# Two graph layers on one core: seven block products for eight in the maps of layer 0, and edges counted by fours

## The chip, the cores and the metric

The kernel runs on one core of a Trainium2 chip. The metric is device time in microseconds, of the whole program. A core has five engines that work beside each other, each through its own queue in order: TensorE (PE; its weight loads are PEld), VectorE (DVE), ScalarE (ACT), GpSimd (POOL) and SyncE (SP, which only issues transfers here). An engine that waits holds up all that stands behind in its queue.

## The reference

`x` is 4096 x 512 in float32, `adj` 4096 x 4096 of 0 and 1 in int32 (about one in 128 set). Layer 0, cut to what matters:

```
keep = (A > 0) & (cumsum(A > 0, axis=1) <= 64)        # the first 64 neighbours of a row
cnt  = keep.sum(axis=1)
xj   = leaky_relu((keep @ X) / max(cnt, 1) @ W_nb.T + b_nb)
xi   = leaky_relu(X @ W_line.T + b_line)
x    = layernorm(X + xi + where(cnt > 0, xj, 0))
```

Layer 1 is attention over the same neighbours: `Wh = h @ W + bW`, scores from two dot products of each row of `Wh`, masked by `adj`, softmax over a row, times `Wh`, then added to its input and normed. Each layer's output has the shape of `x`.

## The kernel before

The rows are cut in 32 blocks of 128 (`NB`), the 512 columns in four chunks of 128 (`NC`). The order of instructions on each engine is the order in which the program writes them (`manual_schedule`); the framework only adds waits. Four stages follow each other on TensorE.

*Maps of layer 0* (the loop over `i` in 32 blocks). As `(keep @ X) @ W_nb.T` is `keep @ (X @ W_nb.T)`, both maps are taken first: `linear(xt, "nb")` gives Y = X W_nb.T, `linear(xt, "line")` the term of the row itself, each with four float32 matmuls of 128x128 by 128x512 into a PSUM bank of `ps_acc` (six banks; `ps_s` has two more). `xt` is the transposed block. Its transpose comes from a load in pieces (`load_turned_x`, four transfers on POOL's queue into one of three `c` tiles) and one VectorE transpose (`turn_x`). Y is kept in SBUF for all 32 blocks as two terms: `y_hi`, cast by ScalarE (L413), and `y_lo`, the rest, by VectorE (L435). The row's own term goes through `line` (bias added on VectorE), `bend` (leaky relu on ScalarE) and `own` (x added on VectorE, then stored to `own_d` on POOL's queue). `load_own_x` loads x for it into one of three `xb` tiles, on POOL's queue too.

*Codes.* Beside the maps, `adj` is turned into one byte per edge, in 64 steps of 128 rows by 2048 columns. `load_adj` (SP) brings 1 MB of int32; `edge` (ScalarE, a steep sigmoid) makes it bf16 0 or 1; `scan` (VectorE) keeps how many neighbours a row has left, at least 2 and counting down from 66, and multiplies it by the edge; `pack` (ScalarE) makes bytes and POOL stores them to `code_d`. So a code is 0 for no edge, over a threshold for one of the first 64, and lower for a later one. `count` takes the number of neighbours from the end of the scans. `codes_until` runs these steps beside the maps until `AHEAD` = 20 are done.

*Neighbour sums* (32 blocks by four groups `s`). `load_kt` brings a block's codes transposed, `make_kt` (ScalarE, L254) turns 128x1024 bytes into 0 or 1 in float32r, and 64 matmuls (L521) add `keep @ y_hi` and `keep @ y_lo` in one bank. `finish` norms a block and stores it. `codes_step` and `codes_late` run the other 45 codes here, at `RATE` = 25/16 a block.

*Layer 1*: maps with W (L825), then attention (L739), where products of pairs of blocks are already taken as seven for eight. The change leaves it as it is.

Before the maps, `turn_w` transposes the weights on TensorE, and `fold_w` (ten VectorE steps of 128x512) folds W with the two score vectors.

Of the kernel before, what the change touches and what calls it, by code (L numbers as in the profile page):

```python
# [9 lines left out]
F32 = mybir.dt.float32  # L10
# [10 lines left out]
P = 128  # L21
# [11 lines left out]
def two_layer_adj_gnn(  # L33
# [43 lines left out]
    two, steep, far, neg_half = few[:, 0:1], few[:, 1:3], few[:, 3:4], few[:, 4:5]  # L77
    for k, value in enumerate((2.0, -0.5 * STEEP, -1.5 * STEEP, FAR, -0.5)):
        nc.vector.memset(few[:, k : k + 1], value)
# [57 lines left out]
    with ExitStack() as l0:  # L137
        adj_p = l0.enter_context(tc.tile_pool(name="l0_adj", bufs=2))
        big = l0.enter_context(tc.tile_pool(name="l0_big", bufs=1))
        y_hi = big.tile([P, NB, C], F32R, name="y_hi")  # L140
        y_lo = big.tile([P, NB, C], F32R, name="y_lo")
# [20 lines left out]

        def edge(s):
            if s < NB * NCH:
                b, h = divmod(s, NCH)
                edge_of[s] = adj_p.tile([P, CH], BF16, name="edge")
                nc.scalar.activation(  # L167
                    edge_of[s], loaded.pop(s), AF.Sigmoid, bias=steep[:, 0:1], scale=STEEP,
# [3 lines left out]
        def scan(s):  # L172
            if s < NB * NCH:
                b, h = divmod(s, NCH)

                left = adj_p.tile([P, CH], BF16, name="left")
                e = edge_of.pop(s)
                end = ends[:, b : b + 1]
                nc.vector.tensor_tensor_scan(  # L179
                    left, two.to_broadcast([P, CH]), e,  # L180
                    NEIGHBORS + 2.0 if h == 0 else end, ALU.max, ALU.subtract,
                )
                nc.vector.tensor_copy(end, left[:, CH - 1 : CH])
                nc.vector.tensor_tensor(left, e, left, ALU.mult)  # L184
                seen_of[s] = left
# [3 lines left out]
        def count(b):  # L189
            two_b = slice(b, b + 2)  # L190
            cnt = stat.tile([P, 2], F32, name="cnt")
            nc.vector.tensor_scalar(cnt, ends[:, two_b], 2.0, -1.0, ALU.max, ALU.mult)
            nc.vector.tensor_scalar_add(cnt, cnt, NEIGHBORS + 2.0)
# [4 lines left out]
        def pack(s):  # L198
            if 0 <= s < NB * NCH:
                b, h = divmod(s, NCH)  # L200
                code = adj_p.tile([P, CH // 2], BF16, name="code")
                nc.scalar.copy(code.bitcast(U8), seen_of.pop(s))  # L202
# [57 lines left out]
        with ExitStack() as la:  # L260
# [3 lines left out]
            AHEAD = 20  # L264
# [28 lines left out]
            def turn_x(i):  # L293
                if i < NB:
                    xts[i] = work.tile([P, NC, P], F32, name="xt", bufs=3)
# [46 lines left out]
            def linear(lhs_t, name):  # L342
                pl = ps_acc.tile([P, C], F32, name="acc")
# [41 lines left out]

            load_own_x(0, nc.sync)
# [8 lines left out]
            spin(12)  # L395
            turn_x(0)
            turn_w("nb", 2)
            for i in range(NB):
                if i > 1:
                    load_own_x(i - 1, nc.gpsimd)  # L400
                if i > 0:
                    load_turned_x(i + 4)
                    turn_x(i + 2)
                xt = xts.pop(i)
                pys[i] = linear(xt, "nb")
                if i == 0:
                    turn_w("line")
# [541 lines left out]
```

## Time and profile before

| | us |
|---|---|
| median of three runs | 1599.97 (1599.85 to 1600.56) |
| profiled execution, its own time | 1600.12 |
| its span, first to last instruction | 1598.4 |
| until the first map (9.6) | 9.6 |
| maps of layer 0 (9.6 to 235.8) | 226.2 |
| neighbour sums (235.8 to 699.8) | 464.0 |
| maps of layer 1 (699.8 to 815.6) | 115.8 |
| attention and end (815.6 to 1598.4) | 782.8 |

In the lines of the profile, a group is: source line, engine, operation, output<-inputs by the program's names, shapes, number; then busy time in us and the mean ns of one; then the idle time of the engine just before them and what ended it. A float32 matmul of the program is two records. A row of busy time by stage has the length, then the busy time of each engine with its number of instructions, the granted clock of TensorE, the share of time in which the DMA engines were busy, and GB/s.

### The profile page before, as it was taken

Reading aid. Unit: us, or ns where it says so; the run is one execution under the profiler, and the core shown is the slowest. Engines: PE = TensorE matmul, PEld = TensorE weight load, DVE = VectorE, ACT = ScalarE, POOL = GpSimd, SP = SyncE. Lnnn points to the kernel's source line nnn. Section 1 sums busy time; section 2 is a strip of 40 time slices with the busy share of each in tenths; the row PEclk is TensorE's granted clock in tenths of the full one; section 3 lists DMA queues with packets and bytes.
Section 4 is the critical chain, followed back from the end, with each engine's and each line's share of the span. In section 5 each row is a group of like instructions: output and inputs, shape, how many; then the busy total and the mean of one; then the engine's idle time right before and its main releaser. Section 6 shows DMA issues by size and latency. Waiting matters only on the chain.

```text
span 1598.4 us, 18483 instructions
## 1 busy us (share of the span) xinstructions
PE 1579.6 (99%) x6456; PEld 1218.4 (76%) x6456; DVE 1305.4 (82%) x2154; ACT 924.2 (58%) x1086; POOL 260.0 (16%) x396
## 2 busy tenths in 40 slices
PE   8999999999999999999999999999999999999997
PEld 4444448888888888864378888888888888888886
DVE  4999986999999999555888887878888888788863
ACT  2655556777777777514237755557755557655520
POOL 4455531122223122210000000000000000000000
PEclk9999999999999999999999999999999999999999
DMA  8887867676757666444201111111111111211100
GB/s 195 287 259 236 265 217 224 215 220 211 229 189 228 206 215 191 116 103 122 76 27 28 53 54 41 52 36 34 53 47 47 48 28 44 54 41 53 40 7 33
DMA packets 168364, 192.73 MB, mean 121 GB/s; under 512 B 101408, under 2 KB 134464, under 8 KB 160080
## 3 DMA queue, kind: packets, MB, share of 16 engines
q1 hardware_dynamic: 147968, 131.38, 29.4%
q0 software_dynamic: 19728, 59.27, 11.0%
q8 instruction: 50, 0.82, 0.2%
q10 hardware_dynamic: 576, 0.92, 0.2%
q14 instruction: 42, 0.34, 0.1%
HBM read 132.65 MB, written 42.08 MB: 109 GB/s over the span
## 4 chain that ended last, share of the span: by engine, by line
PE 92%; DVE 3%; DMA 2%; issue 1%; ACT 1%; SPq 0%; POOL 0%; DVEq 0%; POOLq 0%; ACTq 0%
PE acc L739 34%; PE acc L521 29%; PE pt L739 14%; PE acc L345 9%; PE acc L825 5%; DMA c<-in_x_dram 1%; DVE left L179 1%; DMA a<-in_L_gnn_W_line_dram 1%; DMA edge<-in_L_gnn_a_dram 0%; DVE edge L361 0%; DVE xt L299 0%; DMA w<-x_d 0%; DVE y_lo L435 0%; DVE t L375 0%; ACT w L635 0%
## 5 line engine op out<-in xcount | busy, mean ns | idle before, releaser
L521 PE MATMUL acc<-y_hi,kt 128*128 128x512 f32 x1016 | 395.2, 389 | 0.0
L521 PE MATMUL acc<-y_lo,kt 128*128 128x512 f32 x1016 | 395.2, 389 | 0.0
L739 PE MATMUL acc<-bt,s 128*128 128x256 f32 x1536 | 342.6, 379 | 0.0
L739 PEld LDWEIGHTS acc<-bt,s 128*128 128x128 f32 x1536 | 291.8, 190 | 39.7
L635 ACT ACTIVATE w<-nat,few 128x1024 f32<-128x1024 uint8 x128 | 136.9, 1135 | 290.1 <-DVE a L699 238.8
L126 POOL TENSOR_TENSOR rs<-ve,few 128x1 f32<-128x1 f32 x64 | 76.2, 1191 | 969.3 <-DVE ve L124 969.2
L739 PE MATMUL acc<-bt,a 128*128 128x256 f32 x1024 | 232.1, 379 | 0.0
L739 PE MATMUL pt<-bt,a 128*128 128x256 f32 x1024 | 231.5, 379 | 0.0
L521 PEld LDWEIGHTS acc<-y_hi,kt 128*128 128x128 f32 x1016 | 190.8, 188 | 39.7
L521 PEld LDWEIGHTS acc<-y_lo,kt 128*128 128x128 f32 x1016 | 190.6, 188 | 39.5
L739 PEld LDWEIGHTS pt<-bt,a 128*128 128x128 f32 x1024 | 194.6, 190 | 26.9 <-issue 0.5
L254 ACT ACTIVATE kt<-ktb,few 128x1024 fp32r<-128x1024 uint8 x124 | 142.9, 1152 | 124.7 <-PE acc L521 107.8
L739 PEld LDWEIGHTS acc<-bt,a 128*128 128x128 f32 x1024 | 194.6, 190 | 26.5
L699 DVE STREAM_TRANSPOSE a<-w 128x1024 f32<-128x1024 f32 x128 | 153.0, 1224 | 57.8 <-ACT w L680 53.2
L627 ACT ACTIVATE w<-w,st_n 128x1024 f32<-128x1024 f32 x128 | 149.4, 1233 | 39.5 <-DVE m L638 39.5
L638 DVE CUSTOM_DVE_ANT_0 w<-e_n,w 128x1024 f32<-128x1024 f32 x128 | 149.6, 1221 | 9.6 <-ACT w L635 8.2
L167 ACT ACTIVATE edge<-a,few 128x2048 bf16<-128x2048 int32 x64 | 127.4, 1991 | 43.4 <-DVE left L184 20.3
L680 ACT ACTIVATE w<-w,nm 128x1024 f32<-128x1024 f32 x128 | 145.4, 1136 | 11.3 <-DVE nm L671 11.3
L179 DVE TENSOR_TENSOR_SCAN left<-few,edge 128x2048 bf16<-128x2048 f32 x32 | 141.3, 4415 | 12.7 <-ACT edge L167 10.9
L179 DVE TENSOR_TENSOR_SCAN left<-few,ends,edge 128x2048 bf16<-128x2048 f32 x32 | 143.2, 4475 | 2.3 <-ACT code L202 2.3
L202 ACT CAST code<-left 128x2048 uint8<-128x2048 bf16 x64 | 120.5, 1882 | 0.0
L345 PE MATMUL acc<-wt_nb,xt 128*128 128x512 f32 x256 | 115.5, 594 | 2.8 <-DVE xt L299 2.0
(135 smaller groups left out, 1521.3 us busy)
## 6 DMA issues: line engine op xcount, KB each, us to landing
a<-in_adj_dram SPq DMA_DIRECT2D x64, 1024.0 KB, 5.3
code_d<-code POOLq DMA_DIRECT2D x64, 256.0 KB, 3.7
nat<-code_d SPq DMA_DIRECT2D x256, 64.0 KB, 2.0
own_d<-xb POOLq DMA_DIRECT2D x32, 256.0 KB, 5.9
w<-x_d SPq DMA_DIRECT2D x128, 64.0 KB, 2.0
c<-in_x_dram POOLq DMA_DIRECT2D x124, 64.0 KB, 5.6
xb<-in_x_dram POOLq DMA_DIRECT2D x31, 256.0 KB, 5.8
own<-own_d SPq DMA_DIRECT2D x31, 256.0 KB, 2.8
```

Source lines behind the costliest of these rows:

```text
L167: nc.scalar.activation(edge_of[s], loaded.pop(s), AF.Sigmoid, bias=steep[:, 0:1], scale=STEEP, accum_out=cnts[:, h, b : b + 1],)
L179: nc.vector.tensor_tensor_scan(left, two.to_broadcast([P, CH]), e, NEIGHBORS + 2.0 if h == 0 else end, ALU.max, ALU.subtract,)
L202: nc.scalar.copy(code.bitcast(U8), seen_of.pop(s))
L254: nc.scalar.activation(kts[s], bytes_.rearrange("p t (i r) -> p t r i", r=2), AF.Sigmoid, bias=steep[:, 1:2], scale=STEEP,)
L345: nc.tensor.matmul(pl, lhs_t[:, k, :], w_t[name][:, k, :], start=(k == 0), stop=(k == NC - 1),)
L521: nc.tensor.matmul(accs[i], kt[:, k // 2, k % 2, :], term[:, j, :], start=(j == 0 and term is y_hi), stop=(j == NB - 1 and term is y_lo),)
L627: nc.scalar.activation(dst, src, AF.Prelu, bias=bias, scale=scale, alpha=0.2)
L635: nc.scalar.activation(w_i, nats[b, i // 2].bitcast(U8)[:, i % 2, :], AF.Relu, bias=far, scale=-FAR)
L638: nc.vector.tensor_tensor_reduce(w_i, e2_n, w_i, 1.0, -3e38, ALU.subtract, ALU.max, m4s[b][:, i : i + 1])
L680: nc.scalar.activation(w_i, w_i, AF.Exp, bias=nms[b][:, i : i + 1], accum_out=z4s[g][:, r, i : i + 1])
L699: nc.vector.transpose(a[:, r].rearrange("p s (i a) -> p i s a", a=SQ), wts[2 * g + r][:, :, ts(k, 8 * SQ)].rearrange("p i (s x) -> p i s x ...
L739: nc.tensor.matmul(banks[g][n], lhs[:, j, :], bt[:, 4 * k + j, rhs, :], start=(k == 0 and j == 0 and n == mate[0]), stop=(k == NP - 1 and ...
```

## The change

In the maps of layer 0, blocks 2 to 25 are taken in pairs. A pair's upper and lower block, each in two halves of the 512 inner columns, are a 2x2 matrix of blocks; both weights side by side are another (`w11`, `w21` of W_nb, `w12`, `w22` of W_line). `seven` takes their product with seven products of two matmuls each: sums of the weights (`t1` to `t4`) are made once, sums of x (`s1`, `s2`, `s4`, and `a21` in place) by VectorE for each pair. The sums of products grow in PSUM: a bank is copied to another by ScalarE, or written by VectorE as a sum, and later products are added onto it. `line`'s bias is copied into a bank ahead of a product. A call of `seven` takes the new half of pair `g` and the old half of pair `p` = `g` - 1. Blocks 0, 1 and 26 to 31 are taken one by one as before.

In `scan`, four columns are summed first (planes `p q t` of a tile, made by `edge`'s order of reading), the scan runs over the 512 sums, and the values of single columns are put together again; the counts go from 69 down to at least 5, and the second threshold moves to 4.5. `pack` reads the planes in turn. `AHEAD` goes from 20 to 13, `RATE` from 25/16 to 29/16.

```diff
-    for k, value in enumerate((2.0, -0.5 * STEEP, -1.5 * STEEP, FAR, -0.5)):
+    for k, value in enumerate((5.0, -0.5 * STEEP, -4.5 * STEEP, FAR, -0.5)):
...
+        def fours(t):
+            return t.rearrange("p (q t) -> p q t", q=4)
...
-                edge_of[s] = adj_p.tile([P, CH], BF16, name="edge")
+                edge_of[s] = fours(adj_p.tile([P, CH], BF16, name="edge"))
                 nc.scalar.activation(
-                    edge_of[s], loaded.pop(s), AF.Sigmoid, bias=steep[:, 0:1], scale=STEEP,
+                    edge_of[s], loaded.pop(s).rearrange("p (t q) -> p q t", q=4),
+                    AF.Sigmoid, bias=steep[:, 0:1], scale=STEEP,
...
+        def scan_sums(s):
...
+                left = fours(adj_p.tile([P, CH], BF16, name="left"))
+                e = edge_of[s]
                 end = ends[:, b : b + 1]
+                nc.vector.tensor_tensor(left[:, 0:2], e[:, 0:4:2], e[:, 1:4:2], ALU.add)
+                nc.vector.tensor_tensor(left[:, 2], left[:, 0], left[:, 1], ALU.add)
                 nc.vector.tensor_tensor_scan(
-                    left, two.to_broadcast([P, CH]), e,
-                    NEIGHBORS + 2.0 if h == 0 else end, ALU.max, ALU.subtract,
+                    left[:, 3], five.to_broadcast([P, CH // 4]), left[:, 2],
+                    NEIGHBORS + 5.0 if h == 0 else end, ALU.max, ALU.subtract,
                 )
-                nc.vector.tensor_copy(end, left[:, CH - 1 : CH])
+                nc.vector.tensor_copy(end, left[:, 3, CH // 4 - 1 :])
...
+        def scan_codes(s):
...
+                nc.vector.tensor_tensor(left[:, 1], left[:, 3], left[:, 1], ALU.add)
+                nc.vector.tensor_tensor(left[:, 0:4:2], left[:, 1:4:2], e[:, 1:4:2], ALU.add)
                 nc.vector.tensor_tensor(left, e, left, ALU.mult)
...
-                nc.scalar.copy(code.bitcast(U8), seen_of.pop(s))
+                nc.scalar.copy(
+                    code.bitcast(U8).rearrange("p (t q) -> p t q", q=4),
+                    seen_of.pop(s).rearrange("p q t -> p t q"),
+                )
...
-            AHEAD = 20
+            AHEAD = 13
...
+            def turn_pair(g, r):
+                i = 2 * g + r
+                turn_x(i, (top, low)[r](g) if i < EDGE else None)
+                load_turned_x(i + 3)
+
+            def sums_x(g):
+                a11, a21, a22 = top(g)[:, 0:2], low(g)[:, 0:2], low(g)[:, 2:4]
+                tt(s1, a21, a22, ALU.add)
+                tt(a21, a11, a21, ALU.subtract)
+                tt(s2, s1, a11, ALU.subtract)
+
+            def sum4_x(g):
+                tt(s4, top(g)[:, 2:4], s2, ALU.subtract)
...
+            turn_pair(1, 0)
+            tt(t1, w12, w11, ALU.subtract)
+            tt(t2, w22, t1, ALU.subtract)
+            y_low = y_terms(0, pys[0])
+            load_own_x(1, nc.gpsimd)
+            pys[1] = linear(xts[1], "nb")
+            x_low[1] = xt_tile()
+            turn_pair(1, 1)
+            y_low()
+            line(0)
+            bend(0)
+            pls[1] = linear(xts.pop(1), "line")
...
+            y_low = y_terms(1, pys[1])
+            sums_x(1)
+            own(0)
+            fold_w()
+            y_low()
+            line(1)
+            bend(1)
+            tt(t4, w21, t2, ALU.subtract)
+            tt(w12, w22, w12, ALU.subtract)
+            t3 = w12
+            own(1)
...
+            def seven(g, last, codes):
...
+                if new:
+                    product(x_g, top(g)[:, 0:2], w11, start=True)
+                if old:
+                    y_low = y_terms(2 * p, bank_y)
+                    y_low()
+                if new:
+                    load_own_x(2 * g + 1, nc.gpsimd)
+                    turn_pair(g + 1, 0)
+                    nc.scalar.copy(bank_y, x_g)
+                if old:
+                    product(x_p, low(p)[:, 0:2], t3)
+                codes[0]()
+                if new:
+                    turn_pair(g + 1, 1)
+                    product(bank_z, s1, t1)
+                if old:
+                    tt(tp, tp, x_p, ALU.add)
+                if new:
+                    nc.scalar.copy(tg, bank_z)
+                    nc.scalar.copy(bank_z, bias_line)
+                if old:
+                    nc.scalar.activation(tp, tp, AF.Prelu, alpha=SLOPE)
+                    product(bank_w, s4, w22)
+                codes[1]()
+                if old:
+                    nc.scalar.activation(t0, bank_w, AF.Prelu, alpha=SLOPE)
+                    own_pair(2 * p + 1, tp)
+                if new:
+                    load_own_x(2 * g, nc.gpsimd)
+                    sum4_x(g)
+                    product(x_g, s2, t2)
+                codes[2]()
+                if old:
+                    own_pair(2 * p, t0)
+                if new:
+                    tt(bank_w, tg, x_g, ALU.add)
+                if old:
+                    product(x_p, low(p)[:, 2:4], t4)
+                if new and 2 * g + 2 < EDGE:
+                    sums_x(g + 1)
+                codes[3]()
+                if old:
+                    y_terms(2 * p + 1, x_p)()
+                if new:
+                    product(bank_y, top(g)[:, 2:4], w21)
...
+                if g == 1:
+                    steps = [lambda: (load_adj(0), load_adj(1)), idle[0], idle[0], lambda: edge(0)]
+                elif q < (g - 1) * 10 // 11:
+                    steps = [
+                        lambda: (load_adj(q + 2), edge(q + 1)),
+                        lambda: scan_sums(q),
+                        lambda: pack(q - 1),
+                        lambda: scan_codes(q),
+                    ]
+                    done[0] += 1
+                seven(g, False, steps)
...
+                codes_until(AHEAD if i >= EDGE + 2 else AHEAD - 2 + i - EDGE)
...
-        RATE = 25 / 16
+        RATE = 29 / 16
```

## The prediction

> **What bounds the kernel now.** I read the page's first part, then the chain that ended last, then busy time by stage, then groups and waits inside the two stages that the change touches.
>
> ```profile
> PE 1579.6 (99%) x6456; PEld 1218.4 (76%) x6456; DVE 1305.4 (82%) x2154; ACT 924.2 (58%) x1086; POOL 260.0 (16%) x396
> ```
>
> The chain of waits, in order of time (start, length, what):
>
> ```profile
> 84.44 151.33 PE acc L345 x352
> 235.78 464.03 PE acc L521 x2047
> ```
>
> TensorE carries both stages without a break: the maps of layer 0 until 235.8 us (L345), then the neighbour sums (L521). So a matmul fewer in the maps is time off the end, as long as nothing else becomes late. One block of rows is 8 matmuls, each recorded twice: 352 records are 22 blocks, 151.33/22 = 6.88 us a block, 0.860 us a matmul. (The mean of 594 ns in the groups counts overlap and is no price.) What else could become late stands in busy time by stage (length, then PE, PEld, DVE, ACT, POOL, clock, DMA share, GB/s):
>
> ```profile
> 84.40:235.80 151.40, 151.36 (x353) 67.17 (x354) 144.94 (x158) 83.63 (x93) 78.32 (x142) 1.00 0.79 247
> 235.80:699.80 464.00, 464.00 (x2048) 384.01 (x2047) 396.00 (x500) 328.62 (x290) 102.15 (x109) 1.00 0.65 197
> ```
>
> In the maps VectorE is as full as TensorE (145 of 151 us); in the sums ScalarE has 71%, VectorE 85%. The groups of the sums, for ScalarE's prices:
>
> ```profile
> L254 ACT ACTIVATE kt<-ktb,few 128x1024 fp32r<-128x1024 uint8 x124 | 142.9, 1152 | 124.7 <-PE acc L521 107.8 <-ACT code L202 8.1 <-ACT edge L167 4.8
> L167 ACT ACTIVATE edge<-a,few 128x2048 bf16<-128x2048 int32 x43 | 85.4, 1986 | 0.0
> L202 ACT CAST code<-left 128x2048 uint8<-128x2048 bf16 x45 | 84.7, 1882 | 0.0
> ```
>
> ScalarE's idle time ends mostly on TensorE freeing a `kt`: it is ahead, and has room.
>
> **What the Trainium skill says.** "VectorE: DVE Perf Modes", What auto-detection actually checks: a two-source op runs at two elements a cycle where every tensor is 16-bit with unit step. The product at L184 (2048 bf16, 1225 ns) agrees, and the new adds step over planes only in an outer dimension. "Vector Engine (DVE) Microarchitecture Reference", 5.2 Measured stream behaviour: a VectorE stream that hops at every element takes 1.71 to 1.76 ns a column in place of 1.05, pairs of adjacent words being free; one single-source case ran at full rate. "SBUF — State Buffer", Door 1, on 16-byte lines: "each access that crosses to a new line pays a penalty". No operation of the trace before hops at every element, so nothing here confirms either. "ScalarE: Activation LUTs", What ACT_TABLE_LOAD costs: about 1990 ns for N=2048 with a bias operand; `edge` has 1986.
>
> **The change, part by part.**
>
> *TensorE.* Blocks 2 to 25 are 12 pairs with 7 products of 2 matmuls, 14 for 16; the others are as before. 24 x 0.860 = 20.6 us less, all on the path. `turn_w` for the line weights stays at its place in TensorE's queue.
>
> *VectorE in the pairs.* Consecutive starts in the timeline give 0.62 (transpose), 0.58 (`line`), 0.59 (`own`), 0.60 (`y_lo`). A pair keeps two of each: 4.8 us. Added: four sums of 256 columns at about 0.32 (0.27 of streaming, 0.05 fixed): 1.3. A code took 4.43 (scan) + 0.18 + 1.15 = 5.76. Now the scan has a quarter (about 1.15), the copy 0.18, the product 1.15, the adds two of 1024 (0.61) and two of 512 (0.35): 4.40, and 0.2 for `count`. A pair with a code comes to 10.7 us, against 14 x 0.860 = 12.04 on TensorE.
>
> *ScalarE in the pairs.* Two casts, two bends, three 512-wide copies and one code: 3.8 + 3.8 = 7.6 of 12.04. The new copies into PSUM are priced like the L413 cast (0.57); half or twice that stays hidden.
>
> *Order inside a pair.* Taking TensorE's first product as 0, the seven start 1.72 apart. The tightest needs: the fifth (6.9) wants `bank_y` copied, which ends near 2.5; the sixth (8.6) wants `tt(tp, tp, x_p)`, done at 4.2; the next pair's second wants `bank_w`, done at 9.4, at 13.8. Each has over 4 us, so no product should wait in the steady loop.
>
> *Start.* `fold_w` (ten steps of 0.74, 7.4 us) now stands in VectorE's queue ahead of `line(1)`, behind which are `bend(1)`, the bias copy into `bank_z` and the first pair's third product. `turn_x(3)` must wait until block 0 is multiplied (19.9). From there 0.62 + 0.60 + 0.58 + 0.96 + 0.59 + 7.4 + 0.60 + 0.58 on VectorE and about 1.3 on ScalarE: 33.1. TensorE is there at 26.6 + 1.7 = 28.4: **+4.7**. SP's first adj loads stand behind the store of `wa`, so they start at 31 instead of 24.98, and `edge(0)` is in ScalarE's queue ahead of the second pair's `y_hi`. The first edge came 14.1 us after its load before; again that would be a wait of 3.5, with fewer transfers around it none. I take **+1.8**. The gaps on TensorE at 40 to 60 us before (20.00 less 17.96 busy) went with early scans and late loads of x; there are none so early now: **-2.0**.
>
> *POOL's queue.* It issues 13 transfers a pair at 0.556 (53.5 us/97 in its group): 7.2 us. New is that `xb` has three buffers and two rows are in use: `load_own_x(2g)` follows the store of row 2p+1 whose buffer it takes, and `load_own_x(2g+3)` follows the store of 2p. Each waits on POOL for a store to land; behind it stand the turned loads, for which VectorE's next transposes wait. Landing of `xb` transfers:
>
> ```profile
> DMA to landing us min/median/max: 2.3/5.9/9.2
> ```
>
> The long ones lie beside a 1 MB adj load. Round trip: store 2.4, load and code issued 1.1, second store queued behind both 2.5, then nine issues 5.0: 11.0 us with quiet queues, under 12.04. One adj load per pair adds to it: under the turned loads some 1.5, under a store 5. Turned loads are wanted one to two pairs later, which covers the first. Bounds 0 to 4; I take **+1.5**.
>
> *The neighbour sums.* 13 codes ahead for 20, so 52 in place of 45 fall here, 29/16 a block for 25/16; a block is 464.03/32 = 14.50 us. VectorE: 4.2 for `finish`, 0.4 `count`, 1.81 x 4.40 = 8.0: 12.6, less than the 13.6 before. If the adds ran at one element a cycle they would cost 1.6 more a code, and 15.5 a block. ScalarE by starts: four `kt` at 1.06, a bend 0.53, 1.81 x (edge 2.0 + pack 1.79) = 6.9: 11.6, so 2.9 is left, **1.58 a code**. Here is the unknown. `edge` now reads int32 at 16-byte steps, and `pack` hops among four planes at each element. Lower bound: nothing more (the number of elements is the same, which excludes a gain). Upper: 1.73 ns for the 0.83 of an element, an estimate from the VectorE page: 0.9 x 2048 = 1.84 us on each instruction, 3.7 a code, of which 2.1 is not absorbed. I take nothing, by the single-source case. Both ends are in the range.
>
> Sum: -20.6 - 2.0 + 4.7 + 1.8 + 1.5 = **-14.6**. The profiled span was 1598.4 and that run 1600.1, 0.15 above the median of 1599.97: 1583.8 + 1.7 - 0.15 = 1585.4, said as 1585. Its own range is 1577 to 1592 (all stalls small; or POOL at 4 and the start at 8).
>
> **Rivals.**
>
> *ScalarE becomes the bound in the sums (slower).* With both reads at the upper price, a block takes 11.6 + 1.81 x 3.7 = 18.3 us on ScalarE against 14.5: 3.8 x 28.7 blocks (52 codes at 1.81) = 109, ending at 1585 + 109 = **1694**. It decides from 1.58 extra a code, and outweighs the gain from 1.58 + 14.6/52 = 1.86. For it: two pages of the skill, and a step of exactly one line. Against: the single-source case, and 2-byte hops at L254 cost nothing visible (1152 for 1024 elements), though these stay inside lines.
>
> *Only one of the two reads is dear.* 11.6 + 3.3 = 14.9: 0.45 x 28.7 = 13, **1598**, range 1590 to 1612.
>
> *POOL's round trip meets the adj load under a store.* 16 us a pair in place of 12.04 over ten pairs: +40, **1625**. For it: stores issued just behind an adj load took 6 to 9 us to land. Against: the adj load's start is tied to `edge`, and the loop settles where it lies under the turned loads. The same time would show if the adds missed the double rate (1.0 x 28.7 = 29, so 1614).
>
> That the count of matmuls doesn't fall is excluded by the diff.
>
> **How the numbers follow.** Forecast 0.46, ScalarE as the bound 0.30, one dear read 0.13, POOL or slow adds 0.11. 0.2% is 3.2 us, about what a measurement can tell. Faster takes 0.45 of the first and 0.05 of the third: 0.50; same 0.06; slower 0.44. The forecast, the third and fourth cases hold nearly 0.7; to reach eight in ten the range must go into the ScalarE case up to its middle: 1577 to 1694. Inside it 1577 to 1592 is the likeliest case's own.
>
> **What would show it.** Right: about 464 matmul records in the maps for 512, L521 from about 221 us and 464 long; `edge` and `pack` still near 2.0 and 1.9 us; the scan near 1.15. Wrong: `edge` or `pack` near 3.8 and TensorE waiting at L521 for `kt`; POOL's `xb` load waiting for `own_d` with VectorE's transposes behind it; bf16 adds of 1024 at 1.1 us; a first pair later than 33 us.

## The result, and the profile after

| | before | after |
|---|---|---|
| median of four runs each | 1600.18 us (1599.85 to 1600.56) | **1726.95 us** (1724.51 to 1727.15) |
| ratio | | 1.0789 (95% interval 1.077 to 1.0807) |
| span of the profiled execution | 1598.4 | 1722.7 |
| maps of layer 0 end at | 235.8 | 247.0 (forecast 221.2) |
| neighbour sums take | 464.0 | 577.9 (forecast 464) |
| from there to the end | 898.6 | 897.8 |

The kernel is slower by 127 us where 15 us less was forecast. The time is the first rival's, ScalarE as the bound of the neighbour sums (1694), with 33 us on top. This is the first part of the profile's page, the busy time of each engine:

```profile
PE 1595.4 (93%) x6408; PEld 1205.8 (70%) x6408; DVE 1266.8 (74%) x2463; ACT 1184.3 (69%) x1123; POOL 220.5 (13%) x396
```

Against before, TensorE has 48 matmul records fewer (24 matmuls), as the change says, and VectorE 39 us less. But ScalarE went from 924.2 to 1184.3 us with only 37 instructions more. Here are the maps and the sums in busy time by stage (start and end, length, then PE, PEld, DVE, ACT, POOL with their numbers of instructions, clock, DMA share, GB/s):

```profile
10.90:247.00 236.10, 211.22 (x481) 90.55 (x481) 171.04 (x306) 158.10 (x146) 101.89 (x187) 0.97 0.62 189
247.00:824.90 577.90, 490.35 (x2051) 378.02 (x2050) 389.44 (x738) 545.81 (x311) 68.43 (x119) 1.00 0.59 177
```

In the sums TensorE now has 87.5 us of idle time, and ScalarE is busy for 545.8 of 577.9. The groups say with what (columns as explained under the profile before):

```profile
L737 PE MATMUL acc<-y_hi,kt 128*128 128x512 f32 x824 | 330.7, 401 | 87.5 <-ACT kt L281 87.5
L175 ACT ACTIVATE edge<-a,few 128x2048 bf16<-128x2048 int32 x64 | 255.7, 3995 | 5.8 <-DMA a<-in_adj_dram 5.8
L226 ACT CAST code<-left 128x2048 uint8<-128x2048 bf16 x64 | 247.3, 3864 | 0.0
L281 ACT ACTIVATE kt<-ktb,few 128x1024 fp32r<-128x1024 uint8 x124 | 141.1, 1147 | 21.6 <-PE acc L737 15.3
```

`edge` went from 1986 to 3995 ns and `pack` from 1882 to 3864 ns, while `kt`, untouched, stayed at 1147. Before, ScalarE waited for TensorE to free a `kt`; now TensorE waits for ScalarE to make one. The chain that ended last, in the middle of the sums (start, length, what), runs through ScalarE alone:

```profile
750.23 1.04 ACT kt L281
751.27 3.81 ACT code L226
755.08 2.09 ACT kt L281 x2
757.17 2.98 ACT edge L175
```

The maps don't keep the forecast either: 25.8 us later than forecast. Four of the waits between 40 and 215 us there (who waited <- for what: us in total, times, longest) show more than one cause:

```profile
POOL xb L309 <- DMA own_d<-xb: 64.2, 20, 6.3
ACT acc L551 <- DVE y_lo L419: 23.4, 10, 6.4
PE acc L490 <- DVE acc L578: 11.9, 7, 5.3
DVE xb L413 <- ACT t L564: 10.9, 7, 2.1
```

POOL waits for its own stores, and ScalarE and VectorE for each other. The copy into `bank_y` (L551) comes once a pair; eleven of them start between 51.93 and 186.03 us, so a pair takes 13.4 us and not 12.0.

### The profile page after: what moved, and what is told of

Read it like the earlier page. It is cut to its first block, busy times and chain, and to the rows that moved or that the text cites. A ratio compares the mean times of both kernels' runs of the same rounds, so it can differ in the third digit from the quotient of the medians.

```text
span 1722.7 us, 18790 instructions
## 1 busy us (share of the span) xinstructions
PE 1595.4 (93%) x6408; PEld 1205.8 (70%) x6408; DVE 1266.8 (74%) x2463; ACT 1184.3 (69%) x1123; POOL 220.5 (13%) x396
## 4 chain that ended last, share of the span: by engine, by line
PE 53%; ACT 2%; DVE 1%; issue 0%; DMA 0%; SPq 0%; POOLq 0%; DVEq 0%; ACTq 0%
PE acc L955 32%; PE pt L955 13%; PE acc L1041 5%; PE acc L737 3%; ACT code L226 1%; ACT kt L281 0%; DMA w<-x_d 0%; DVE c L805 0%; ACT edge L175 0%; ACT lm L843 0%; SPq L791 0%; ACT w L851 0%; DVE bt L814 0%; DVE w L854 0%; ACT w L896 0%
## 5 line engine op out<-in xcount | busy, mean ns | idle before, releaser
L737 PE MATMUL acc<-y_hi,kt 128*128 128x512 f32 x824 | 330.7, 401 | 87.5 <-ACT kt L281 87.5
L737 PE MATMUL acc<-y_lo,kt 128*128 128x512 f32 x824 | 321.7, 390 | 0.0
L737 PEld LDWEIGHTS acc<-y_hi,kt 128*128 128x128 f32 x824 | 154.5, 188 | 153.5 <-ACT kt L281 123.1
L175 ACT ACTIVATE edge<-a,few 128x2048 bf16<-128x2048 int32 x64 | 255.7, 3995 | 5.8 <-DMA a<-in_adj_dram 5.8
L226 ACT CAST code<-left 128x2048 uint8<-128x2048 bf16 x64 | 247.3, 3864 | 0.0
L915 DVE STREAM_TRANSPOSE a<-w 128x1024 f32<-128x1024 f32 x128 | 153.0, 1224 | 57.8 <-ACT w L896 53.2
L737 PEld LDWEIGHTS acc<-y_lo,kt 128*128 128x128 f32 x824 | 154.8, 188 | 30.0
L126 POOL TENSOR_TENSOR rs<-ve,few 128x1 f32<-128x1 f32 x64 | 38.6, 604 | 926.6 <-DVE ve L124 926.4
L896 ACT ACTIVATE w<-w,nm 128x1024 f32<-128x1024 f32 x128 | 145.4, 1137 | 11.2 <-DVE nm L887 11.2
L193 DVE TENSOR_TENSOR left<-edge 128x1024 bf16<-128x1024 bf16 x64 | 44.0, 687 | 90.9 <-ACT code L226 90.9
L1041 PE MATMUL acc<-w,c 128*128 128x512 f32 x232 | 102.0, 601 | 2.6 <-DVE c L805 2.6
L1041 PEld LDWEIGHTS acc<-w,c 128*128 128x128 f32 x232 | 44.5, 192 | 59.9 <-issue 53.7
```

What stands on the lines that cost most here:

```text
L175: nc.scalar.activation(edge_of[s], loaded.pop(s).rearrange("p (t q) -> p q t", q=4), AF.Sigmoid, bias=steep[:, 0:1], scale=STEEP, accum_ou ...
L193: nc.vector.tensor_tensor(left[:, 0:2], e[:, 0:4:2], e[:, 1:4:2], ALU.add)
L226: nc.scalar.copy(code.bitcast(U8).rearrange("p (t q) -> p t q", q=4), seen_of.pop(s).rearrange("p q t -> p t q"),)
L737: nc.tensor.matmul(accs[i], kt[:, k // 2, k % 2, :], term[j], start=(j == 0 and term is y_hi), stop=(j == NB - 1 and term is y_lo),)
L896: nc.scalar.activation(w_i, w_i, AF.Exp, bias=nms[b][:, i : i + 1], accum_out=z4s[g][:, r, i : i + 1])
L915: nc.vector.transpose(a[:, r].rearrange("p s (i a) -> p i s a", a=SQ), wts[2 * g + r][:, :, ts(k, 8 * SQ)].rearrange("p i (s x) -> p i s x ...
```

## The experiments

Two theories were set against each other first: that the two hopping reads on ScalarE (`edge` at steps of 16 bytes, `pack` among four planes) cost double and are all of the loss, and that the pairs in the maps have a loss of their own beside it, which stays when the reads are in order. Where no interval is given, a time is that of a single run.

### Both reads in order, the counts follow the planes

`edge` makes plane `q` from a quarter of the columns and not from every fourth, so it reads in order, and `pack` writes the planes one after the other. Sizes and numbers of instructions are the same.

```diff
-                    edge_of[s], loaded.pop(s).rearrange("p (t q) -> p q t", q=4),
+                    edge_of[s], loaded.pop(s).rearrange("p (q t) -> p q t", q=4),
...
-                    code.bitcast(U8).rearrange("p (t q) -> p t q", q=4),
-                    seen_of.pop(s).rearrange("p q t -> p t q"),
+                    code.bitcast(U8).rearrange("p (q t) -> p q t", q=4),
+                    seen_of.pop(s),
```

> The kernel after, with edge and pack reading and writing in order (neighbours are then counted in the order of the planes and not of the columns, which the text of the experiment says; every other instruction is the same). Theory S, ScalarE's hopping reads are the whole loss: edge and pack fall from 4.0 and 3.9 to 2.0 and 1.9 us, the neighbour sums from 578 to 464 us, the pairs from about 14 to 12.0 us each, and the time is 1585 to 1595. Rival P, the order and the buffer waits inside a pair cost on their own: the sums fall to 464, but the pairs stay near 14 us and the time is 1610 to 1620. Rival V, VectorE's adds are slow: the sums stay above 480 us.

It took 1619.15 us (1617.68 to 1622.51), 1.0119 of before (1.0102 to 1.0136). `edge` is at 2.00 and `pack` at 1.89 us. Busy time by stage:

```profile
9.30:253.30 244.00, 214.30 (x481) 92.09 (x481) 171.79 (x307) 108.43 (x146) 103.62 (x190) 0.95 0.62 189
253.30:718.10 464.80, 464.80 (x2051) 384.82 (x2050) 385.87 (x738) 354.60 (x311) 68.60 (x116) 1.00 0.74 218
```

The sums are back at 464.8 us, TensorE full in them: the reads are the whole of that stage's loss, 113.1 us. But the kernel is still slower than before, and that lies in the maps, which end later still with 50 us less on ScalarE: a pair takes 14.8 us, from the same copies. So reads alone don't explain the result: the maps have a loss of their own, and the time is the one that the second theory gave.

### One read hopping at a time

Each is the kernel above with one of its two edits taken back. A row's codes then no longer stand in the order of its columns; sizes and numbers of instructions stay the same.

> The kernel after, only pack in order (codes then land in the order of the planes). Theory S with ScalarE's room of 1.6 us a code in the sums: the edge's 2.0 us more passes it by 0.4, so some 52 x 0.4 = 21 us over the run with both in order: 1605 to 1620. If each read cost its own full 2.0 us times 65 codes, half of the loss would stay: about 1655.

> The kernel after, only edge in order (the counts then follow the order of the planes). As for the edge alone: pack's 2.0 us more passes ScalarE's room in the sums by 0.4 a code, 1605 to 1620; with no room about 1655. If hops among four planes were cheap, as for a single stream between two regions, pack would be at 1.9 us and the time that of both in order.

Only `edge` hopping took 1625.76 us, only `pack` 1637.18. In each, the hopping read's group between 270 and 700 us, first the kernel with `edge` hopping:

```profile
L175 ACT ACTIVATE edge<-a,few 128x2048 bf16<-128x2048 int32 x49 | 198.4, 4049 | 0.0
```

then the one with `pack` hopping:

```profile
L226 ACT CAST code<-left 128x2048 uint8<-128x2048 bf16 x52 | 204.8, 3938 | 0.0
```

The instruction that reads in order is at 1961 ns (`pack`) and 1994 ns (`edge`) in them. The sums took 478.8 and 482.0 us, so 14.0 and 17.2 more; both together 113.1. The costs don't add, because ScalarE's room is used once: a read adds 2.0 us to a code, of which (14.0 to 17.2)/52 = 0.27 to 0.33 is not absorbed; two add 4.0, of which 113.1/52 = 2.2 is not. So the room is 1.7 to 1.8 us a code, where the prediction had 1.58. What was expected of these two was too low by 6 and 17 us: it was worked out from a lower time for the kernel with both in order, and the maps, which end at 249.1 and 255.6 us, still hold their own loss.

### The hopping reads in the kernel before

No seven products, no fours: only the order of reading.

```diff
-                    edge_of[s], loaded.pop(s), AF.Sigmoid, bias=steep[:, 0:1], scale=STEEP,
+                    edge_of[s].rearrange("p (q t) -> p q t", q=4),
+                    loaded.pop(s).rearrange("p (t q) -> p q t", q=4), AF.Sigmoid, bias=steep[:, 0:1], scale=STEEP,
...
-                nc.scalar.copy(code.bitcast(U8), seen_of.pop(s))
+                nc.scalar.copy(
+                    code.bitcast(U8).rearrange("p (t q) -> p t q", q=4),
+                    seen_of.pop(s).rearrange("p (q t) -> p q t", q=4),
+                )
```

> The kernel before, with edge and pack reading in the hopping order of the kernel after and nothing else of the change (edge's columns and scan's order are then permuted, and the counts follow that order). Theory S: edge and pack go to 4.0 and 3.9 us; the sums go to 10.7 + 1.56 x 4.0 = 16.9 us a block for 28.8 blocks, some 70 us more, and the maps some 10 more: 1670 to 1690. If the hops hurt only in the new order, about 1600 to 1610.

It took 1660.53 us. Groups between 270 and 700 us:

```profile
L203 ACT CAST code<-left 128x2048 uint8<-128x2048 bf16 x41 | 160.0, 3903 | 0.0
L167 ACT ACTIVATE edge<-a,few 128x2048 bf16<-128x2048 int32 x40 | 157.5, 3938 | 0.0
```

The price belongs to the reads, whatever stands around them. The loss is 60 us and not 126: 45 codes fall in the sums here for 52, and a block leaves ScalarE more room (60/45 = 1.3 us of a code's 4.0 is not absorbed). That is 10 us under what was expected.

### A fourth buffer for the x of the pairs

In the kernel with both reads in order, POOL's waits between 30 and 215 us:

```profile
POOL xb L309 <- DMA own_d<-xb: 75.2, 20, 6.8
```

`load_own_x` waits for the store of a row whose buffer it takes, and the turned loads stand behind it. The timeline of the same kernel shows where that goes (start, length, engine, line, what; in brackets the idle time before it and what ended it):

```profile
104.33 0.57 POOL L309 DMA_DIRECT2D xb<-in_x_dram  x1 [3.01 <-DMA own_d<-xb]
108.65 0.69 DVE L413 TENSOR_TENSOR xb<-xb,lo 128x512 f32<-128x512 f32 x1 [2.94 <-DMA xb<-in_x_dram]
109.26 0.69 DVE L578 TENSOR_TENSOR acc<-t,acc 128x512 f32<-128x512 f32 x1
110.00 3.26 PE L490 MATMUL acc<-wt_line,lo 128*128 128x512 f32 x4 [2.13 <-DVE acc L578]
110.07 0.55 POOL L309 DMA_DIRECT2D xb<-in_x_dram  x1 [4.11 <-DMA own_d<-xb]
```

POOL issues a load of x late, since it waited for a store. VectorE waits for that x at `own`, the sum into `bank_w` stands behind `own` in its queue, and TensorE waits for the bank. A fourth buffer lies free in this stage, in `room_lo`.

```diff
+            own_tiles = [work.tile([P, C], F32, name="xb", bufs=3) for _ in range(3)]
+            own_tiles.append(room_lo[:, 5])
...
-                    load_own_x(2 * g + 1, nc.gpsimd)
+                    load_pair_x(2 * g + 1)
```

The same is done for `2 * g`; `load_pair_x` takes the four tiles in turn.

> The kernel after with edge and pack in order (counts follow the planes) and a fourth buffer in the ring of xb, in a part of a tile that stood empty. Theory R, POOL's round trips bound the pairs: POOL's waits for own_d fall from 73 us to under 20, a pair from 14.6 to 12.0 to 12.5 us, and the time from 1619 to 1590 to 1597. Rival Y, the order on VectorE and ScalarE bounds the pairs (the cast rest y_lo stands behind the codes, the copy of a bank behind y_lo): POOL waits less, but the pairs stay above 13.5 us and the time above 1608.

It took 1588.67 us, 30.5 less, and just under what was expected. POOL's wait between 30 and 190 us, and busy time in the middle of the maps:

```profile
POOL xb L309 <- DMA own_d<-xb: 10.5, 8, 1.9
```

```profile
100.00:150.00 50.00, 50.00 (x118) 22.08 (x117) 46.73 (x84) 32.84 (x45) 30.12 (x56) 1.00 0.75 241
```

TensorE runs without a gap for 50 us, and ten pairs take 118.1 us (the copies into `bank_y` from 50.52 to 168.64), 11.8 each, where 14 x 0.860 is 12.0. So with the reads in order, the round trip through POOL's queue was what held the pairs, and not the order of the instructions in them. The maps end at 224.3.

A wait of TensorE cost more here than its own length. From the first map to the end of the maps it is 212.5 us for 244.0, and some 10 of these 31.5 us are not waits but busy time, 204.24 us for 214.30 in the same matmuls, at a mean granted clock of 0.98 for 0.95. In the timeline above, the four records after the wait of 2.13 us took 3.26 us; four that followed others without a wait (98.98 in the same trace) took 1.88.

The same buffer in the changed kernel, reads still hopping:

> The kernel after with only the fourth xb buffer. If POOL's round trips and ScalarE's hops hold the pairs each for itself, the pairs fall from 14.1 to about 13 us (ScalarE has 4 + 4 + 3.8 us a pair then, near TensorE's 12.0), the sums stay at 578: 1705 to 1718. If the hops alone hold the pairs, nothing changes: 1722 to 1730. If only POOL did, 12.0 to 12.3 us a pair: 1695 to 1704.

It took 1719.24 us, only 7.7 less and a little over what was expected. A pair still takes 13.1 us. Between 100 and 150 us ScalarE is busy for 41.6 of 50:

```profile
100.00:150.00 50.00, 46.64 (x106) 19.18 (x104) 40.84 (x75) 41.60 (x38) 26.66 (x50) 1.00 0.66 208
```

In time, the two causes make a square:

| | three buffers | four buffers |
|---|---|---|
| reads hop | 1726.95 | 1719.24 |
| reads in order | 1619.15 | 1588.67 |

The buffer is worth 7.7 or 30.5, the reads 107.8 or 130.6. Either cause alone holds the pairs at 13 us or more; only when both are gone do they come to 12.

### `fold_w` behind the first pair

The fourth buffer kept, the ten `fold_w` steps go from ahead of the first pair to between the steps of the second, and the first `edge` with them.

```diff
             own(0)
-            fold_w()
             y_low()
...
-                    steps = [lambda: (load_adj(0), load_adj(1)), idle[0], idle[0], lambda: edge(0)]
+                    steps = [lambda: (load_adj(0), load_adj(1)), idle[0], idle[0], idle[0]]
+                elif g == 2:
+                    steps = [idle[0], fold_w, idle[0], lambda: edge(0)]
```

> Edge and pack in order (counts follow the planes), the fourth xb buffer, and fold_w moved behind the first pair. If the 5.4 us gap ahead of the first pair is fold_w in VectorE's queue, it shrinks to under 1.5 us and the time from 1589 to 1583 to 1586; if the gap is x of the second block coming late, it stays and the time is 1588 to 1590.

It took 1583.06 us, 5.6 less, as expected. In the timeline of the changed kernel TensorE stands still for 4.84 us ahead of the first pair, for the `y_lo` that is behind `fold_w` on VectorE:

```profile
32.90 3.68 PE L490 MATMUL acc<-wt_nb,xt 128*128 128x512 f32 x4 [4.84 <-DVE y_lo L419]
```

That gap is gone here. But not all of the 5.6 us belongs to it. The first map started at 11.83 us in the run without this edit and at 9.45 in this one, and two executions of one and the same later kernel differ as well (9.41 and 10.80), so 2.4 us are the start of the execution. From the first map to the end of the maps it is 209.2 us for 212.5, 3.3 less: where `fold_w` now stands TensorE has new waits, 4.0 us for the sum into `bank_w` (L585). This kernel has about the time of the prediction, 1585, but with a fourth buffer and without the start's +4.7.

### Hopping writes in place of hopping reads

If a read at steps of 16 bytes is dear, can the write hop? `edge` reads in order and writes its bf16 to the four planes in turn (1024 bytes apart); `pack` reads in order and writes bytes four apart.

```diff
-                    edge_of[s], loaded.pop(s).rearrange("p (t q) -> p q t", q=4),
+                    edge_of[s].rearrange("p q t -> p t q"),
+                    loaded.pop(s).rearrange("p (t q) -> p t q", q=4),
...
-                    code.bitcast(U8).rearrange("p (t q) -> p t q", q=4),
-                    seen_of.pop(s).rearrange("p q t -> p t q"),
+                    code.bitcast(U8).rearrange("p (t q) -> p q t", q=4),
+                    seen_of.pop(s),
```

> The kernel after, with edge and pack reading in order and writing in hops (bf16 1024 bytes apart, bytes 4 apart); it computes what the kernel after does. If only reads pay for hops: 2.0 and 1.9 us, and 1615 to 1625 as with both in order. If writes pay as reads do: 4.0 and 3.9 us and 1715 to 1735. If bytes 4 apart share a word's price, pack alone is cheap: 1620 to 1640.

It took 1985.6 us, beyond all three expectations. Groups between 320 and 1060 us:

```profile
L175 ACT ACTIVATE edge<-a,few 128x2048 bf16<-128x2048 int32 x50 | 479.2, 9584 | 0.0
L227 ACT CAST code<-left 128x2048 uint8<-128x2048 bf16 x52 | 128.8, 2476 | 0.0
```

A bf16 write that hops 1024 bytes at every element takes 9.6 us for 2048, more than twice the hopping read. Byte writes four apart are cheap, 2.48.

### The seven products with the old scan

Is counting by fours needed at all? Here the scan is that of before (one column at a time, reads in order), with the fourth buffer and `fold_w` behind the first pair. More codes are made ahead; in the second kernel `own`'s sum goes to POOL too (there `AHEAD` is 16 and `RATE` 55/32).

```diff
-                nc.vector.tensor_tensor(left[:, 0:2], e[:, 0:4:2], e[:, 1:4:2], ALU.add)
-                nc.vector.tensor_tensor(left[:, 2], left[:, 0], left[:, 1], ALU.add)
                 nc.vector.tensor_tensor_scan(
-                    left[:, 3], five.to_broadcast([P, CH // 4]), left[:, 2],
-                    NEIGHBORS + 5.0 if h == 0 else end, ALU.max, ALU.subtract,
+                    left, two.to_broadcast([P, CH]), e,
+                    NEIGHBORS + 2.0 if h == 0 else end, ALU.max, ALU.subtract,
                 )
...
-            AHEAD = 13
+            AHEAD = 15
...
-        RATE = 29 / 16
+        RATE = 28 / 16
```

> Seven products with the scan over single columns of the kernel before (AHEAD 15, RATE 28/16), the fourth xb buffer, and fold_w moved behind the first pair. Theory R: the pairs at 12.1 to 12.6 us (VectorE: 6.1 + 5.8 a pair), the first pair starts 4 us earlier than in the kernel after, the sums at 464 to 472 us (VectorE at 101% of TensorE's 14.5 us a block): 1582 to 1594. Rival Y: pairs above 13.5 us, above 1600.

> The same with own's sum on POOL in place of VectorE, AHEAD 16 and RATE 55/32. It takes 0.59 us twice a pair from VectorE: if VectorE is what holds the pairs then, 2 to 6 us under the run without it. If POOL's sum takes over 1.5 us each, POOL's queue (7.2 us of issues a pair) has over 10 of 12 us and the turned loads come late: 5 us or more above it.

They took 1613.38 and 1625.1 us. In the first, VectorE holds up the sums; busy time of a stretch in them:

```profile
400.00:500.00 100.00, 95.87 (x407) 78.33 (x406) 94.23 (x114) 73.72 (x67) 25.17 (x23) 0.97 0.68 215
```

They take 485 us for 464.8, with VectorE busy for 94% of this stretch and 88% of the whole: TensorE waits for `kt`, and ScalarE, which makes it, waits for VectorE's `t` (85.9 us in 21 waits). The maps end at 229.0, with one gap of 8 us where the transpose of a block stands behind three scans of 4.4 us on VectorE. In the second the gap is 14 us, the twelve copies into `bank_y` span 144.1 us for 134.7, and the maps end at 248.3. Most of POOL's sums of 128x512 took 1.28 us, where VectorE has 0.69; their mean was 1.7 and the longest took 4.93.

The first was expected to gain over the kernel before and lost; the second lost as its own second case says. With fewer matmuls, TensorE leaves VectorE less time for the same work. With these two settings of `AHEAD` and `RATE`, the lighter scan is a condition of the gain; others were not tried.

### Counting by twos

Two planes in place of four: `edge` reads at steps of 8 bytes, one add of 1024 makes the sums, the scan runs over 1024 of them, one add puts the first column of each pair together, and `pack` either reads in order and writes bytes two apart, or reads two planes in turn and writes in order.

```diff
+                nc.vector.tensor_tensor(left[:, 0], e[:, 0], e[:, 1], ALU.add)
                 nc.vector.tensor_tensor_scan(
-                    left[:, 3], five.to_broadcast([P, CH // 4]), left[:, 2],
-                    NEIGHBORS + 5.0 if h == 0 else end, ALU.max, ALU.subtract,
+                    left[:, 1], three.to_broadcast([P, CH // 2]), left[:, 0],
+                    NEIGHBORS + 3.0 if h == 0 else end, ALU.max, ALU.subtract,
                 )
...
+                nc.vector.tensor_tensor(left[:, 0], left[:, 1], e[:, 1], ALU.add)
                 nc.vector.tensor_tensor(left, e, left, ALU.mult)
...
-                    code.bitcast(U8).rearrange("p (t q) -> p t q", q=4),
-                    seen_of.pop(s).rearrange("p q t -> p t q"),
+                    code.bitcast(U8).rearrange("p (t q) -> p q t", q=2),
+                    seen_of.pop(s),
```

With the fourth buffer and `fold_w` behind the first pair:

> It computes what the kernel after does, but counts by twos: edge reads every second int32 (8-byte steps), the scan has 1024 sums, and pack reads two planes in order and writes bytes 2 apart; with the fourth xb buffer and fold_w behind the first pair. If the price is per 16-byte line (two of four words of a line are used in turn), edge stays at 2.0 us; pack writes 4 apart took 2.5 us, so 2 apart takes 1.9 to 2.2: ScalarE has room, VectorE 4.8 us a code, and the time is 1583 to 1592. If the price is per 8-byte pair, edge is at 3.5 to 4.0 us and the sums take 480 us or more: 1600 to 1625.

> The same with pack reading two planes in turn and writing in order. If a hop between two streams is free (as the single-source case of the skill's VectorE page), pack is at 1.9 us and the time within 4 us of the run with hopping writes; if every hop is paid, pack is at 3.9 us and the time 15 us or more above it.

It took 1577.47 us with hopping writes, some 6 us better than expected, and 1578.08 with hopping reads, which is no difference that a single run can tell. ScalarE's groups between 240 and 690 us, first writes:

```profile
L175 ACT ACTIVATE edge<-a,few 128x2048 bf16<-128x2048 int32 x48 | 101.6, 2117 | 0.0
L221 ACT CAST code<-left 128x2048 uint8<-128x2048 bf16 x51 | 96.5, 1893 | 0.0
```

then reads from two planes:

```profile
L221 ACT CAST code<-left 128x2048 uint8<-128x2048 bf16 x51 | 109.1, 2138 | 0.0
```

A step of 8 bytes costs 6%, two planes in turn 13%, bytes two apart nothing. The first of the two was then timed again, beside the kernel before:

> The version by twos with the fourth xb buffer and fold_w behind the first pair, now timed: 1576 to 1580, 1.3% to 1.5% under the kernel before.

**It took 1578.98 us (1577.79 to 1579.92), 0.986 of before (0.9843 to 0.9876).** It is faster than both kernels, and 21.8 us faster than the one before. Its maps take 205.4 us, where the 226.2 of before less the 20.6 forecast for 24 matmuls are 205.6. Busy time by stage:

```profile
9.40:214.80 205.40, 201.97 (x478) 88.97 (x479) 173.62 (x282) 110.08 (x146) 103.98 (x191) 1.00 0.76 224
214.80:680.00 465.20, 465.20 (x2051) 384.77 (x2051) 396.67 (x636) 361.12 (x312) 76.49 (x116) 1.00 0.72 218
```

Two more say what carries it. Counting by twos in the changed kernel, with its three buffers and early `fold_w`:

> The kernel after counting by twos and nothing else changed. If ScalarE's hops and POOL's round trips are separate causes, this stays with the round trips: pairs near 14.5 us, sums 464, 1612 to 1622. If the reading order was the one cause: 1580 to 1592.

It took 1619.25 us, as with both reads in order (1619.15), and POOL waits again:

```profile
POOL xb L304 <- DMA own_d<-xb: 75.4, 20, 6.9
```

And counting by twos in the kernel before, without seven products:

> The kernel before with the scan by twos and nothing else. If the gain is TensorE's 24 matmuls, a lighter VectorE changes nothing here: 1597 to 1602. If VectorE's load held the maps before, 1585 to 1595.

It took 1599.57 us against 1600.81, which is no gain that a single run can tell. VectorE's lighter scan is worth nothing by itself where TensorE sets the time, and the seven products gained nothing without it as they were tried. Together, with the hopping reads and POOL's round trip gone, they are worth what the matmuls take.

## Why the prediction was wrong, step by step

The account is made against the forecast for the span, 1583.8. Measured 1722.7, so +138.9: the sums 577.9 for 464.0 (forecast as before), +113.9; the maps' end 247.0 for 221.2, +25.8, of which 1.2 is a later first map (10.86 for 9.62); the rest 897.8 for 898.6, -0.8.

**The hopping reads: "I take nothing, by the single-source case". This step failed, and in the sums alone it is 113 of the 139 us.** The reads cost 2.01 and 1.98 us more each, 4.0 a code. The prediction's upper bound was 1.84 each with 2.1 not absorbed; measured 2.2 is not. The working of the rival stood: 464 + 109 = 573 for the sums, 577.9 measured. Over its 28.7 blocks with codes that is 14.5 + 113.9/28.7 = 18.5 us a block for 18.3. It was the choice between two bounds that was wrong. The chosen one came from one case on VectorE, whose stream alternates between two regions: two planes in turn are near it here (2.14 us for 1.88), but the change had four planes, and a step of a whole line. The hops at L254, which the prediction itself had noted to stay inside lines, were no evidence for hops that leave one at each element. At a step of exactly one line the Trainium skill's page "SBUF — State Buffer" (Door 1) had said that each crossing pays. The runs agree with its rule that a line needs two accesses or more for full bandwidth: two int32 of each line take 2.12 us, one takes 4.0. They don't agree with its reading that fp32 can be strided by four for free, if that means a step of four; and two planes in turn, which cross at every element as well, are nearly free, while four planes take 3.86, which the line alone doesn't explain. The skill's "Vector Engine (DVE) Microarchitecture Reference", 5.2, gives 1.71 to 1.76 ns a column for hops of 4 KiB on one operand or both sources, and 2.50 for steps of 24 words, which the prediction left out. ScalarE's was 1.95 ns (3995/2048) for the int32 at 16-byte steps, so the 1.73 taken as the upper bound was near, and low. A chance of 0.30 was too little for a rival with two pages for it and nothing in this kernel's traces against it.

**POOL's queue: "+1.5", bounds 0 to 4. This failed too.** Removing the wait was worth 30.5 us with reads in order. The prediction had followed the wait to the right place (POOL's `xb` load waiting for `own_d`) and had found 11.0 us in quiet queues against 12.04: 1 us of slack. In the trace of the kernel with reads in order POOL waits 20 times, 75.2/20 = 3.8 us each and up to 6.8, and a pair takes 14.8 us. What was mis-sized is the round trip's stores: it put 2.4 and 2.5 us for them and took a late adj load as falling "under the turned loads". In the same trace a store of `own_d` took 3.6 us to land on the median and up to 11.6; the prediction's own line of the landings had a median of 5.9. Its last rival (16 us a pair, 1625) named this, and 1619.15 was measured with reads in order. The prediction also followed the wait to VectorE's transposes, whereas the trace leads through `own`: VectorE waits for x itself (26.6 us in eight waits), ahead of the sum that TensorE needs. The time for that load to land was no term of its round trip.

**The order inside a pair: "Each has over 4 us, so no product should wait in the steady loop".** This held when the two causes were gone (pairs of 11.8 us), and failed in the changed kernel: with three buffers or four, a pair took over 13 us as long as the reads hopped. The kernel with four buffers and hopping reads shows the way it was lost, between two copies into `bank_y` (L559), the first at 88.47 us:

```profile
88.95 4.04 ACT L175 ACTIVATE edge<-a,few 128x2048 bf16<-128x2048 int32 x1
94.76 0.69 DVE L413 TENSOR_TENSOR xb<-xb,lo 128x512 f32<-128x512 f32 x1 [2.09 <-ACT lo L572]
100.36 1.28 DVE L419 TENSOR_TENSOR y_lo<-acc,y_hi 128x512 fp32r<-128x512 f32 x2
101.73 0.57 ACT L559 COPY acc<-acc 128x512 f32<-128x512 f32 x1 [1.86 <-DVE y_lo L419]
```

ScalarE works without a gap from that copy through `edge` and two copies to the leaky relu (L572, until 94.72). `own` on VectorE (L413) waits for it, and VectorE then works without a gap until the two `y_lo` end at 101.64; the next copy waits for these. This is one chain through both queues, 13.3 us long, once a pair. Of the two reads only `edge` stands in it: `pack` runs beside VectorE, and ScalarE still waits 1.86 us after it. Without `edge`'s 2.0 us more the chain is some 11.3, an estimate from these figures, and fits under TensorE's 12.04. The runs with one hopping read agree. With `edge` alone hopping, four copies in a row stand 13.3 us apart (60.82 to 100.59). With `pack` alone they come 11.9 and 11.2 apart from 50.77 to 73.94, much as with both in order (11.7 and 11.2), and slow down later as these do. So the step had each need held against TensorE's times, and not the length of the chain that runs through the two other queues.

**The start: "+4.7".** The gap was right in cause and size: 4.84 us, by `fold_w` in VectorE's queue. TensorE lost it at the first pair's first product, which waited for `y_lo`, and not at its third by way of the bias copy. What the sum had no term for is that TensorE then ran slower: the first four records after the gap took 3.5 us (32.90 to 36.38) where four take 1.7, at a granted clock of 0.57 from 33 to 37 us. The +1.8 and the -2.0 fit roughly: with both reads in order and four buffers, the second pair waits 1.20 us for a copy behind the first `edge` and 1.12 for a sum on VectorE, and after 60 us TensorE has no gap in the maps.

**TensorE: "-20.6".** Right: 24 matmuls fewer, and 50 us of pairs without a gap. The version by twos gains 21.8 us over before, and the scan by twos alone gave no gain that could be told.

**VectorE: right that it has room, and low in price.** The adds of 1024 took 687 to 692 ns and those of 512 416 to 425: 512 elements more cost 0.27 us, 0.52 ns each, against 0.60 for the product that the prediction leaned on. That agrees with the Trainium skill's "VectorE: DVE Perf Modes" (What auto-detection actually checks): the double rate is kept though the planes step in an outer dimension. The scan was 1224 to 1284 ns for 1150. With the product and the copy a code has 4.86 us of busy time for 4.40 forecast, which VectorE's room took in. Groups of the changed kernel between 230 and 800 us:

```profile
L208 DVE TENSOR_TENSOR left<-left,edge 128x1024 bf16<-128x1024 bf16 x52 | 36.0, 692 | 1.8
L195 DVE TENSOR_TENSOR_SCAN left<-few,ends,left 128x512 bf16<-128x512 f32 x26 | 33.4, 1284 | 0.9
```

The maps of the changed kernel end 6 us earlier than those with both reads in order (247.0 and 253.3), although both wait for POOL. That follows `edge`: from the first map on they take 236.1 us, with only `edge` hopping 237.6, with only `pack` hopping 243.6 and with neither 244.0. How a slower `edge` helps there is open: a later adj load under fewer stores would do it, but no run was made for that.

## What to carry to other kernels

Moving a cost from a full engine to one with idle time pays only for so much as that engine has idle in the same stage, so an access pattern new to it needs its price before the order of the data is chosen: here counting by twos kept nearly all of ScalarE's price and about four fifths of VectorE's gain (5.07 us of busy time a code for 4.86 by fours and 5.83 before), while counting by fours doubled two instructions. When blocks are taken in pairs, count again the buffers that were enough for one at a time, and follow each load that waits for a store through the whole queue with the landing times of the trace, not the best one. When two engines wait for each other in turn, add up the chain through both queues and hold that against the bottleneck's time. And a gain of a few matmuls comes out only when the other engines fit into the shorter time: here, in the settings tried, neither the seven products nor the lighter scan gained anything without the other.

## What the runs showed of the hardware

For ScalarE, 128x2048 elements of one instruction, in us:

| access | in order | by twos | by fours |
|---|---|---|---|
| int32 read (steps of 8 and 16 bytes), bf16 written in order | 1.99 | 2.12 | 4.00 |
| bf16 read from planes in turn, bytes written in order | 1.88 | 2.14 (two planes) | 3.86 (four planes) |
| bytes written apart, bf16 read in order | 1.88 | 1.89 | 2.48 |
| bf16 written to planes in turn, int32 read in order | 1.99 | not tried | 9.58 (1024 bytes apart) |

The last row was the surprise: the hopping write is dearer than any read, 4.7 ns an element. Whether the distance, the plane count or the 2-byte size makes it so was not tried. By twos, everything that was tried cost at most 0.26 us.

TensorE's longer waits cost clock as well. Four matmul records take 1.7 us in a row in the maps. After every gap of 3.4 us or more (up to 13.7) in the maps of ten of these kernels, the next ones took 2.5 to 3.6 us for four; after gaps of up to 1.8 us, 1.8 to 2.0; from 1.9 to 3.3 us both happened (2.13: 3.1; 2.86: 1.8), and what decides there was not looked for.
